# Layernorm's root and inverse as a power on GpSimd, and the recurrence's additions one pair later, in a two-layer transformer kernel

## The chip, the cores and the metric

The kernel runs on one core of a Trainium2 chip. The metric is the time of one execution on the device in microseconds (us), as the median of several runs. All arithmetic is in float32. Engines are called as in the profile: PE (TensorE), ACT (ScalarE), DVE (VectorE), POOL (GpSimd), SP (the engine that issues most DMAs).

## The reference, cut to what matters

```python
def _layernorm(x, axis=-1, eps=1e-05):
    m = jnp.mean(x, axis=axis, keepdims=True)
    v = jnp.var(x, axis=axis, keepdims=True)
    return (x - m) / jnp.sqrt(v + eps)

x = L0_attn_x                                       # (4, 2048, 256)
xn = _layernorm(x)
x = x + recurrence(xn) + attention_of_4_chosen_heads(xn)      # layer 0
xn = _layernorm(x)
x = x + causal_attention_16_heads(xn) + channel_mix(xn)       # layer 1
```

The recurrence is `y[t] = a[t] * y[t-1] + b[t]` over the 2048 tokens of a batch, with `a` and `b` from two matrix products, tanh, exp and a square root. The layer-0 attention takes the 4 best of 16 heads for each batch (64 columns each, 2048 by 2048 scores, softmax with the row's maximum subtracted). The layer-1 attention is causal, with 16 heads of 16 columns. The channel mix is `sigmoid(xr W_r) * (relu(xk W_k)^2 W_v)`, where `xr` and `xk` blend a token with the one before it.

## The kernel before, in words

**Order.** The whole program is traced under `in_order`, which ties each of PE, ACT, DVE and POOL to the order in which the Python code issues its instructions. So the order of the work on each engine is written out by hand: Python generators ("streams") are advanced by `steps(stream, count)`, each `yield` ending one step. DMAs on SP follow the order of issue too. The four batches run one after the other.

**Layer 0 attention, `attention0`.** A tile is 128 queries of one chosen head (`Tile0`), a pair is two tiles (`Pair0`). The loop runs over `n`, 0 to 33: pairs 0 to 31 (4 heads, 8 pairs each) and two more rounds that finish what is behind. In round `n` the pair `new` has tiles `a` and `c`; `before` is the pair of round `n-1`, `older` that of `n-2`. A round goes: transposes of the second tile of `before` (`late.turn`, L520, copied out of PSUM by `late.keep`, L526, two by DVE and two by ACT); reciprocals of its sums (L530, L531); output projection of `older` (`project`, L558) and its addition to `x` (`add`, L563); scores of `a` (L498) and their maxima on DVE (L502, combined by L506 into `nm`); exponentials of `a` on ACT (L512); scores of `c`; the product with the values of `before` (`weigh`, L545); exponentials of `c`; transposes of `a` and their copies. The start of a round can be seen in the trace as the `nm` (L506) of its tile `a`. Scores, transposes and projections take seven of the eight PSUM banks in turn, so each waits until the bank's previous user has been read.

Three streams are woven into these rounds. `background` is the recurrence of the same batch, of which 26 of 35 steps are done before round 0: the step for `y + added` of the second half (L330) and eight steps that transpose `y` (L337) and add it to `x` (L339) remain, at two steps a round. `rest_of_values` is the second half of the values' projection (`values0`, L446, copied by L448), four units in round 0. `norming` is `all_blocks`, from round 27 on, at four steps a round: the layernorm for layer 1, in four blocks of 512 tokens.

**Norm.** `stats` takes mean and variance of a tile of 128 tokens (L257, L258). `root` is a Sqrt on ACT with eps as bias (L261), `inverse` a reciprocal on DVE (L265), `rows` writes (x - mean) * inverse for each of four tiles (L272), and `turn` transposes 512 tokens by 128 columns (L278) and copies them (L279). In `all_blocks` a block takes eight steps, two rounds: root in the third, after the exponentials of `a`; inverse and rows in the fourth, after the copies of `a`; the two turns in the first two steps of the next round, one before `late.turn` and one after `late.keep`. Exp and Sqrt are in different tables of ACT, so a change of function is preceded by an ACT_TABLE_LOAD, which has the line of the instruction that it is for.

**Elsewhere.** Layer 0's norm is the same class: for batch 0 at the start of the program, for the others woven into the last head group of layer 1 of the batch before (`prepared`; two steps at a time), with one root and one inverse for all 16 tiles. In `opening1`, woven into the last rounds, `heads.open` fills tiles on POOL (L711, 128x2048) and `values1` fills others (L726); `heads.copy` then copies into them by DMAs from SP (L717). `Maxima` (L772, with L775 or L778) runs ahead for layer 1 in the same stage. In layer 1's late stage POOL also squares `ka` (L983) and adds `sg` (L1011).

Of the kernel before, what the change touches and what calls it, by code (L numbers as in the profile page):

```python
# [10 lines left out]
FP = mybir.dt.float32  # L11
BF = mybir.dt.bfloat16
U32 = mybir.dt.uint32
AF = mybir.ActivationFunctionType
ALU = mybir.AluOpType
# [3 lines left out]
P = 128  # L19
QB = 512  # L20
EPS = 1e-5
# [46 lines left out]
def steps(stream, count):  # L68

    for _ in range(count):  # L70
        if next(stream, StopIteration) is StopIteration:
            return False
    return True
# [3 lines left out]
def two_layers(ctx: ExitStack, tc: tile.TileContext, x, Wa, Wx, ba, bx, Lam,  # L77
# [4 lines left out]
    PE, ACT, DVE, POOL, SP = nc.tensor, nc.scalar, nc.vector, nc.gpsimd, nc.sync  # L82
# [3 lines left out]
    NT = T // P  # L86
    NQ = T // QB
# [7 lines left out]
    const = ctx.enter_context(tc.tile_pool(name="const", bufs=1))  # L95
# [37 lines left out]
    def rows_of(both, n, count):  # L133
# [13 lines left out]
    POOL.memset(cmask, 0.0)  # L147
    POOL.affine_select(out=cmask[:, QB - P:QB], in_=cmask[:, QB - P:QB], compare_op=ALU.is_ge, fill=MASKED,
                       base=0, pattern=[[-1, P]], channel_multiplier=1)
    eps_c = const.tile([P, 1], FP, tag="eps", name="eps_c")  # L150
    POOL.memset(eps_c, EPS)
    quarter_c = const.tile([P, 1], FP, tag="quarter", name="quarter_c")
    POOL.memset(quarter_c, 0.25)
    heads_row = const.tile([P, NH], FP, tag="heads_row", name="heads_row")
# [91 lines left out]
    class Norm:  # L246
# [10 lines left out]
            DVE.bn_stats(self.st[:, t, :], rows_of(self.xt, t, 1)[:, 0, :])  # L257
            DVE.bn_aggr(self.mv[:, t, :], self.st[:, t, :])  # L258

        def root(self, t, n):  # L260
            ACT.activation(self.rs[:, t:t + n], self.mv[:, t:t + n, 1:2].rearrange("p n o -> p (n o)"),  # L261
                           AF.Sqrt, bias=eps_c)

        def inverse(self, t, n):
            DVE.reciprocal(self.rs[:, t:t + n], self.rs[:, t:t + n])  # L265

        def rows(self, q, i0, i1):
            if i0 == 0:
# [182 lines left out]
    def queries0(b, k, xT, ch, bank):  # L451

        qs = [half_tile(f"q0_{b}_{k + i}") for i in range(2)]

        def stream():
            for q in range(NQ):
                blk = slice(q * QB, (q + 1) * QB)
                ps = bank()
                for c in range(2):
                    PE.matmul(ps, lhsT=ch.wq[k // 2][:, c, :], rhs=xT[c][:, blk], start=(c == 0), stop=(c == 1))  # L460
                ACT.activation(qs[0][:, blk], ps, AF.Identity, bias=ch.bias_q[:, k // 2:k // 2 + 1])
                for i in range(2):
                    SP.dma_start(qs[1][i * DH:(i + 1) * DH, blk], qs[0][(1 - i) * DH:(2 - i) * DH, blk])
                yield
        return qs, stream()

    def keys0(b, k, xT, ch, bank):

        kT = c4.tile([P, HT], FP, tag="k0", name=f"k0_{b}_{k}", bufs=2)

        def stream():
            for j in range(NJ):
                ps = bank()
                for c in range(2):
                    for i in range(2):
                        k0 = i * HT + j * QB
                        PE.matmul(ps[i * DH:(i + 1) * DH, :], lhsT=ch.wk[k][:, c, :], rhs=xT[c][:, k0:k0 + QB],  # L477
                                  start=(c == 0), stop=(c == 1))
                ACT.activation(kT[:, j * QB:(j + 1) * QB], ps, AF.Identity, bias=ch.bias[:, 1, k:k + 1])
                yield  # L480
        return kT, stream()
# [83 lines left out]
    def attention0(b, xT, xt, ch, recurring, first, v, rest_of_values, norm, opening, leading):  # L565


        NP = NT // 2
        qk, following = first, None
        background, projecting, norming = recurring, iter(()), iter(())  # L570
        older, before = None, None
        summing[0] = True

        def all_blocks():


            for q in range(NQ):
                yield
                yield
                norm.root(4 * q, 4)  # L580
                yield
                norm.inverse(4 * q, 4)
                norm.rows(q, 0, 2)
                norm.rows(q, 2, 4)
                yield
                for c in range(2):
                    norm.turn(q, c, ACT.copy)
                    yield
                yield
                yield  # L590

        for n in range(NA * NP + 2):
            k, i = divmod(n, NP)
            if i == 0 and 0 < k < NA:
                steps(projecting, 100)
                qk = following
            new = Pair0(b, k, i, *qk, v, xt) if k < NA else None
            a, c = new.tiles if new else (None, None)
            if i == NP - 3 and k + 1 < NA:
                if k % 2:  # L600
                    qs, querying = queries0(b, k + 1, xT, ch, bank)
                else:
                    qs, querying = qk[0], iter(())
                kT, keying = keys0(b, k + 1, xT, ch, bank)
                following = qs, kT
                projecting = concat(querying, keying)
            if n == (NA - 1) * NP + 3:
                norming = all_blocks()

            steps(background, 1)  # L610
            steps(projecting, 1)
            steps(norming, 1)

            if n in (NA * NP - 3, NA * NP - 1) or n >= NA * NP:
                steps(opening, 2)
            if n >= NA * NP:
                leading.lead()
            if before:
                late = before.tiles[1]
                late.turn(1)  # L620
                late.turn(0)
                late.keep(1, 0, DVE.tensor_copy)
                late.keep(0, 0, DVE.tensor_copy)
                late.keep(0, 1, ACT.copy)
                late.keep(1, 1, ACT.copy)
                for tile_ in before.tiles:
                    tile_.share()
            steps(background, 1)
            steps(projecting, 1)
            steps(norming, 1)  # L630
            if older:
                older.project()
                older.add()
                if n - 2 >= (NA - 1) * NP:
                    for t in range(2):
                        norm.stats(2 * (n - 2 - (NA - 1) * NP) + t)
            if before and new is None:
                leading.lead()
            if new:
                a.scores(0)  # L640
                a.scores(1)
                a.exponentials((0, 1))
                steps(rest_of_values, 4)
            steps(norming, 1)
            if new:
                c.scores(1)
            if n >= NA * NP:
                steps(opening, 1)
            if before:
                if new is None:  # L650
                    leading.lead()
                before.weigh(0)
            if new:
                c.scores(0)
                c.exponentials((1, 0))
            if before:
                if new is None:
                    leading.lead()
                before.weigh(1)
            if new:  # L660
                a.turn(1)
                a.turn(0)
                a.keep(1, 0, DVE.tensor_copy)
                a.keep(0, 0, DVE.tensor_copy)
                a.keep(1, 1, ACT.copy)
            if before:
                before.weighed()
            if new:
                a.keep(0, 1, ACT.copy)
            steps(norming, 1)  # L670
            older, before = before, new
        steps(background, 100)
        summing[0] = False
        for _ in range(8):
            steps(opening, 1)
            leading.lead()
            steps(norming, 1)
        steps(norming, 100)
# [336 lines left out]
    def prepared(b, ready):  # L1015

        xt = load_x(b)
        norm = Norm(xt, f"0_{b}", own_bank)
        ch = Chosen()
        ready.append((xt, norm.xT, ch))  # L1020

        def go():
            for t in range(0, NT, 2):
                norm.stats(t)
                norm.stats(t + 1)
                yield
            norm.root(0, NT)
            yield
            norm.inverse(0, NT)
            for q in range(NQ):  # L1030
                norm.rows(q, 0, 2)
                yield
                norm.rows(q, 2, 4)
                yield
                yield
                for c in range(2):
                    norm.turn(q, c, DVE.tensor_copy)
                    yield
        return go(), choose(b, norm.xT, ch)
# [3 lines left out]
    with in_order(tc):  # L1043
# [3 lines left out]
        for b in range(B):  # L1047
# [20 lines left out]
            x1, norm = xt, Norm(xt, f"1_{b}", bank)  # L1068
# [37 lines left out]
```

## Time and profile before

| | us |
|---|---|
| median of 3 runs | 4234.19 (4233.68 to 4235.58) |
| the profiled execution's own time | 4234.65 |
| its span, first to last instruction | 4232.9 |
| ACT table loads in it, 58 of 1.283 each | 74.4 |
| of these for the norms' Sqrt (L261), 20 | 25.7 |
| L506 to L506 of the same tile of the next round, rounds 6 to 10 | 11.82 |
| the same, rounds 27 and 29 | 15.78 |

The profile is of one execution. "Busy" is the time in which an engine ran instructions; the brackets at a row's end in a timeline are the idle time of the engine before it and what ended it. The stages of the four batches repeat almost to the hundredth of a microsecond, so one batch (the second, from about 1151 us) is read in detail, and times inside it are counted from the span's start.

### The profile page before, as it was taken

To read this page: it belongs to the slowest core of one execution; us is meant where nothing else is said; L and a number is where in the kernel's file an instruction comes from. 1 tells how busy PE (TensorE), PEld (TensorE's weight loads), DVE (VectorE), ACT (ScalarE), POOL (GpSimd) and SP (SyncE) were. 2 spreads that over 40 slices of the span, in tenths; PEclk is the share of its full clock that TensorE was granted. 3 is DMA by queue.
4 is the path that set the end of the run, shared out by engine and by line. 5 is a ranking of instruction groups with operands and counts; after the bars stand their busy time and mean duration, and the time that the engine had idled before them with its cause. 6 is when DMAs were issued, how large, how long until landed. Compare 5 with 4: busy or idle time off the path is not lost.

```text
span 4232.9 us, 86387 instructions
## 1 busy us (share of the span) xinstructions
PE 4129.7 (98%) x32994; PEld 2283.5 (54%) x32994; DVE 3107.5 (73%) x7292; ACT 2797.4 (66%) x6388; POOL 1044.9 (25%) x1322
## 2 busy tenths in 40 slices
PE   6999999999999999999999999999999999999998
PEld 3777643334477764333457776433446777643334
DVE  5777778887577777888657776888856767688882
ACT  3666648886566665888656665688865666568874
POOL 0000015544100002654410000265440000036544
PEclk9999999999999999999999999999999999999999
DMA  3000010100100001110010000011000000001000
GB/s 87 1 11 1 6 18 17 19 25 17 27 1 11 1 6 19 17 37 6 19 25 1 11 1 9 16 17 37 7 19 23 1 11 1 16 11 17 16 7 24
DMA packets 70819, 65.80 MB, mean 16 GB/s; under 512 B 37234, under 2 KB 58628, under 8 KB 68868
## 3 DMA queue, kind: packets, MB, share of 16 engines
q1 hardware_dynamic: 66624, 57.19, 6.2%
q8 instruction: 260, 4.26, 0.4%
q10 hardware_dynamic: 3780, 3.07, 0.3%
q14 instruction: 155, 1.27, 0.1%
HBM read 16.70 MB, written 8.39 MB: 6 GB/s over the span
## 4 chain that ended last, share of the span: by engine, by line
PE 90%; DVE 5%; ACT 2%; issue 1%; POOL 1%; DMA 1%; ACTq 0%; SPq 0%; POOLq 0%; DVEq 0%
PE bank L797 15%; PE bank L772 13%; PE bank L808 12%; PE bank L520 11%; PE bank L498 10%; PE bank L545 10%; PE bank L993 4%; PE bank L703 3%; PE bank L294 3%; PE bank L558 2%; DVE mx L778 1%; PE bank L477 1%; PE bank L460 1%; PE bank L981 1%; DVE mx L502 1%; ACT p L512 1%
## 5 line engine op out<-in xcount | busy, mean ns | idle before, releaser
L799 ACT ACTIVATE p<-bank 128x512 f32<-128x512 f32 (+3 forms) x2560 | 1175.4, 540 | 281.1 <-PE bank L797 146.5
L772 PE MATMUL bank<-k,q 32*128 32x512 f32 (+3 forms) x5120 | 1139.1, 564 | 3.2 <-DVE mx L778 1.3
L778 DVE TENSOR_REDUCE mx<-bank 128x1 f32<-128x512 f32 x1536 | 952.9, 682 | 239.0 <-PE bank L772 238.6
L797 PE MATMUL bank<-q,k 32*128 32x512 f32 (+3 forms) x5120 | 1089.6, 555 | 0.0
L512 ACT ACTIVATE p<-bank,nm 128x512 f32<-128x512 f32 x1024 | 689.5, 685 | 568.6 <-DVE nm L506 568.5
L815 POOL TENSOR_TENSOR o<-o,w 128x512 f32<-128x512 f32 (+3 forms) x576 | 627.6, 1090 | 757.5 <-ACT w L814 752.0
L502 DVE TENSOR_REDUCE mx<-bank 128x1 f32<-128x512 f32 x1024 | 645.3, 681 | 94.8 <-PE bank L498 94.2
L797 PEld LDWEIGHTS bank<-q,k 32*128 32x128 f32 x5120 | 418.4, 184 | 533.7 <-ACT p L799 445.5
L808 PE MATMUL bank<-p,v 128*17 128x512 f32 (+3 forms) x5120 | 602.9, 534 | 16.6 <-POOL p L802 11.7
L526 DVE COPY pT<-bank 128x512 f32<-128x512 f32 x512 | 352.6, 691 | 293.2 <-PE bank L520 277.6
L545 PEld LDWEIGHTS bank<-pT,v 128*64 128x64 f32 x8192 | 441.9, 137 | 189.8 <-issue 189.3
L498 PE MATMUL bank<-k,q 64*128 64x512 f32 x2048 | 542.5, 611 | 0.8
L775 DVE CUSTOM_DVE_ANT_0 bank<-bank,cmask 128x512 f32<-128x512 f32 (+3 forms) x1024 | 473.3, 521 | 75.0 <-PE bank L772 56.4
L520 PE MATMUL bank<-ident,p 128*128 128x128 f32 x4096 | 492.3, 275 | 19.9 <-ACT p L512 19.7
L545 PE MATMUL bank<-pT,v 128*64 128x128 f32 x8192 | 503.7, 276 | 0.0
L772 PEld LDWEIGHTS bank<-k,q 32*128 32x128 f32 x5120 | 426.7, 183 | 136.7 <-DVE mx L778 34.5
L520 PEld LDWEIGHTS bank<-ident,p 128*128 128x128 f32 x4096 | 445.3, 141 | 73.8 <-ACT p L512 29.8
L711 POOL MEMSET q<- 128x2048 f32 x16 | 28.9, 1804 | 1659.5 <-PE bank L545 1659.5
L814 ACT COPY w<-bank 128x512 f32<-128x512 f32 (+3 forms) x576 | 305.1, 530 | 101.9 <-PE bank L808 68.4
L526 ACT COPY pT<-bank 128x512 f32<-128x512 f32 x512 | 293.4, 600 | 63.5 <-PE bank L520 61.5
L808 PEld LDWEIGHTS bank<-p,v 128*17 128x17 f32 x5120 | 89.7, 95 | 431.1 <-ACT p L799 235.8
L498 PEld LDWEIGHTS bank<-k,q 64*128 64x128 f32 x2048 | 210.5, 188 | 170.7 <-issue 84.9
(164 smaller groups left out, 3354.8 us busy)
## 6 DMA issues: line engine op xcount, KB each, us to landing
x<-in_L_attn_x_dram SPq DMA_DIRECT2D x20, 512.0 KB
q<-q SPq DMA_DIRECT2D x64, 128.0 KB
vals<-o SPq DMA_DIRECT2D x256, 32.0 KB
out_dram<-x SPq DMA_DIRECT2D x32, 256.0 KB
q<-qp SPq DMA_DIRECT2D x48, 128.0 KB
k<-kp SPq DMA_DIRECT2D x48, 128.0 KB
q<-nmT SPq DMA_DIRECT2D x256, 2.0 KB
q<-qp SPq DMA_DIRECT2D x64, 32.0 KB
```

The costliest lines, as they stand in the source:

```text
L498: PE.matmul(self.s[j][i], lhsT=self.qT[i][half_, self.t * P:(self.t + 1) * P], rhs=self.kT[half_, j * QB:(j + 1) * QB], start=True, stop=True)
L502: DVE.tensor_reduce(self.mx[:, n:n + 1], self.s[j][i], AX.X, ALU.max)
L512: ACT.activation(self.p[j][:, i, :], self.s[j][i], AF.Exp, bias=nm, accum_out=self.sums[:, n:n + 1])
L520: PE.transpose(self.tr[j][i][:, n * P:(n + 1) * P], self.p[j][:, i, n * P:(n + 1) * P], ident)
L526: copy(self.pT[:, n0:n0 + 4, :], self.tr[j][i].rearrange("p (n q) -> p n q", q=P))
L545: PE.matmul(acc[i * DH:(i + 1) * DH, 0:P], lhsT=self.v[h][:, N * j + n, self.k * DH:(self.k + 1) * DH], rhs=tile_.pT[:, 8 * h + N * j + n, ...
L772: PE.matmul(s[:, 0:n], lhsT=self.qT[strip(h), self.qs], rhs=self.kT[strip(h), self.ks], start=True, stop=True)
L778: DVE.tensor_reduce(self.mx[:, h, :], s[:, 0:n], AX.X, ALU.max)
L797: PE.matmul(s[:, c0:QB], lhsT=self.kT[strip(h), self.ks], rhs=self.qT[strip(h), self.q0 + c0:self.q0 + QB], start=True, stop=True)
L799: ACT.activation(p[:, h % 2, c0:QB], s[:, c0:QB], AF.Exp, scale=SC1)
L808: PE.matmul(acc[32 * h:32 * h + DH1 + 1, c0:QB], lhsT=self.v[h], rhs=self.p[h // 2][:, h % 2, c0:QB], start=True, stop=True)
L815: POOL.tensor_tensor(self.o[:, c0:QB], self.o[:, c0:QB], w[:, c0:QB], ALU.add)
```

## The change

The norm's `root` method is gone. `inverse` now adds eps on DVE and raises the sum to the power -0.5 on POOL, in place. In `all_blocks` it stands where the root stood, in the third step, and `rows` stays in the fourth; for the first three blocks the two turns are put together behind `late.keep`, and the fourth keeps the old steps. In round 0 the recurrence's stream and half of the values' units are held back: the stream starts in round 1, and two of the four units come after the exponentials of `c`. 39 ACT_TABLE_LOADs fall out of the program with the 20 roots; one small tile of constants is set up in place of another.

```diff
-    eps_c = const.tile([P, 1], FP, tag="eps", name="eps_c")
-    POOL.memset(eps_c, EPS)
+    minus_half = const.tile([P, NT], FP, tag="minus_half", name="minus_half")
+    POOL.memset(minus_half, -0.5)
...
-        def root(self, t, n):
-            ACT.activation(self.rs[:, t:t + n], self.mv[:, t:t + n, 1:2].rearrange("p n o -> p (n o)"),
-                           AF.Sqrt, bias=eps_c)
-
         def inverse(self, t, n):
-            DVE.reciprocal(self.rs[:, t:t + n], self.rs[:, t:t + n])
+            rs = self.rs[:, t:t + n]
+            DVE.tensor_scalar(rs, self.mv[:, t:t + n, 1:2].rearrange("p n o -> p (n o)"), EPS, None, ALU.add)
+            POOL.tensor_tensor(rs, rs, minus_half[:, 0:n], ALU.pow)
...
             for q in range(NQ):
                 yield
                 yield
-                norm.root(4 * q, 4)
-                yield
                 norm.inverse(4 * q, 4)
+                yield
                 norm.rows(q, 0, 2)
                 norm.rows(q, 2, 4)
                 yield
+                if q < NQ - 1:
+                    yield
                 for c in range(2):
                     norm.turn(q, c, ACT.copy)
-                    yield
+                    if q == NQ - 1:
+                        yield
+                yield
                 yield
                 yield
...
-            steps(background, 1)
+            if n:
+                steps(background, 1)
...
-            steps(background, 1)
+            if n:
+                steps(background, 1)
...
-                steps(rest_of_values, 4)
+                steps(rest_of_values, 2)
...
                 before.weigh(1)
+            steps(rest_of_values, 2)
...
-            norm.root(0, NT)
+            norm.inverse(0, NT)
             yield
-            norm.inverse(0, NT)
             for q in range(NQ):
```

More of the change, by code (lines that the diff above doesn't have):

```diff
@@ L579, in all_blocks @@
                 yield
-                norm.root(4 * q, 4)
+                norm.inverse(4 * q, 4)
                 yield
-                norm.inverse(4 * q, 4)
                 norm.rows(q, 0, 2)
```

## The prediction

> **What bounds the kernel now.** First the page's engine shares:
>
> ```profile
> PE 4129.7 (98%) x32994; PEld 2283.5 (54%) x32994; DVE 3107.5 (73%) x7292; ACT 2797.4 (66%) x6388; POOL 1044.9 (25%) x1322
> ```
>
> PE's 98% is modelled and counts waits inside its pipeline, so I read the touched rounds instead. By windows (columns: length, then busy us of PE, weight loads, DVE, ACT, POOL, the granted clock, DMA), round 26 has no norm block and round 27 has one; otherwise they do the same:
>
> ```profile
> 1486.57:1499.44 12.87, 12.82 (x117) 8.95 (x117) 10.16 (x24) 7.78 (x21) 1.81 (x1) 1.00 0.01 2
> 1499.44:1515.22 15.78, 14.47 (x120) 10.02 (x122) 11.73 (x29) 11.61 (x26) 1.81 (x1) 1.00 0.00 1
> ```
>
> The block costs 15.78 - 12.87 = 2.91 us in this round. The timeline of ACT shows a hole of that size between the exponentials of tile a and those of tile c:
>
> ```profile
> 1502.26 0.21 ACT L512 ACTIVATION_READ_ACCUMULATOR p<-bank,nm 128x1 f32 x1
> 1502.49 1.28 ACT L261 ACT_TABLE_LOAD   x1
> 1503.79 0.30 ACT L261 ACTIVATE rs<-mv,eps_c 128x4 f32<-128x4 f32 x1
> 1504.10 1.28 ACT L512 ACT_TABLE_LOAD   x1
> 1505.40 0.69 ACT L512 ACTIVATE p<-bank,nm 128x512 f32<-128x512 f32 x1
> ```
>
> From 1502.49 to 1505.40 are 2.91 us: a round is a loop of latency, ACT's exponentials, PE's transposes, DVE's copies, additions and maxima, ACT again. DVE's timeline of the same round shows who waits:
>
> ```profile
> 1505.11 0.69 DVE L526 COPY pT<-bank 128x512 f32<-128x512 f32 x1 [0.18 <-PE bank L520]
> 1505.72 0.17 DVE L265 RECIPROCAL rs<-rs 128x4 f32<-128x4 f32 x1
> 1505.92 1.38 DVE L272 TENSOR_SCALAR xn<-x,mv,rs 128x256 f32<-128x256 f32 x4
> 1508.33 0.69 DVE L526 COPY pT<-bank 128x512 f32<-128x512 f32 x1 [1.03 <-PE bank L520]
> ```
>
> The rows lie inside the wait for ACT. Without the loads they are what is late next.
>
> **Rounds 27 and 29.** In round 26 the four copies start 4.80, 5.67, 6.54 and 7.42 us after its L506, each 0.18 behind PE. Without the loads, copies 1 and 2 stand at 4.80 and 5.67 again, the rows run from 6.30 to 7.68 (1.38), and copies 3 and 4, which PE has ready by then, follow back to back at 7.65 and 8.26, ending at 8.95 against 8.11. The round is 12.87 + 0.84 = 13.7, and 2.1 is gained. The turns (8 transposes, 1.0 us by L520's 3.71 for 32) now stand between late.turn and the projection: PE leaves late.turn at 7.74, the turns at 8.75, the projection (0.70) at 9.45, while DVE's additions are ready at 9.38: covered to within 0.1, and up to 0.5 dearer if their banks come late. Their two ACT copies (0.61 each) fall into ACT's 4 us wait for the next maxima.
>
> **Round 31.** There PE waited 1.23 for the exponentials of c behind the loads, then for rows, and L732 started 8.1 us after its L506. Without loads or an early turn, PE is through the transposes of a at 6.0: 2.1 gained. The later turns cost 0.5 beside DVE work that runs without a gap.
>
> So the three blocks give 2.1 + 2.1 + 2.1 = 6.3 a batch. The Exp load at L799 in the opening stage stands before an idle stretch of 3.15: nothing.
>
> **A rule on the loads.** The Trainium skill ("ScalarE: Activation LUTs", What ACT_TABLE_LOAD costs) puts a switch at 2.66 us with a drain of 1.38. The trace shows 1.283 and 0.02 between the last exponential and the load: no drain. By the page the hole would be 5.6 and the gain of a round 4.8; the round grew by only 2.91, so the row decides.
>
> **Round 0.** DVE's timeline of the second batch:
>
> ```profile
> 1143.49 2.47 DVE L330 TENSOR_SCALAR y<-y,added 128x2048 f32<-128x2048 f32 x2
> ...
> 1148.04 1.29 DVE L502 TENSOR_REDUCE mx<-bank 128x1 f32<-128x512 f32 x2 [1.31 <-PE bank L498]
> 1149.75 1.29 DVE L502 TENSOR_REDUCE mx<-bank 128x1 f32<-128x512 f32 x2 [0.42 <-PE bank L498]
> 1151.07 0.16 DVE L506 TENSOR_REDUCE nm<-mx 128x1 f32<-128x4 f32 x1
> ```
>
> PE sat idle for 4.73 before the y transposes at 1144.92, with the scores queued behind them, and then ran slowly (the last column but two is the clock):
>
> ```profile
> 1145.00:1150.00 5.00, 5.00 (x14) 2.12 (x15) 3.20 (x5) 0.00 (x0) 0.00 (x0) 0.54 0.01 3
> ```
>
> Now the scores follow the values at 1140.2 at full clock (1.99 instead of 3.78) and are ready early. DVE does one L330 (half of 2.47), to 1144.73, then four maxima (2.48): L506 at 1147.2, 3.9 earlier. Two values' units (1.8 each) then fill PE while ACT works; scores of c wait for the banks of a's exponentials until about 1150.2, the other two units end at 1153.8, the transposes of a at 1155.7. DVE copies (1.3), does the other L330 (1.24) to 1157.2, copies again (1.3), reciprocals (0.6), one L339 (0.7), and its maxima end at 1162.4. Before, round 1's L506 stood at 1169.03: 6.6 gained. What was moved is paid later: from L506 to L506 it is 12.78 into round 3 with two steps of the stream, 12.39 into round 4 with one, 11.82 into round 6 with none. Round 4 gets a second step (0.4), round 5 one beside the keys (0.6). Net 5.6 a batch. If PE still falls to the slow clock, the two units and c's scores cost up to 4 more: 1.6 to 5.6. SP's order is unchanged; no DMA moves.
>
> **The power.** The trace has none. POOL's two-input rows bound it:
>
> ```profile
> L815 POOL TENSOR_TENSOR o<-o,w 128x512 f32<-128x512 f32 x384 | 487.9, 1271 | 661.1 <-ACT w L814 659.5 <-ACT p L799 0.5
> ...
> L815 POOL TENSOR_TENSOR o<-o,w 128x128 f32<-128x128 f32 x64 | 29.1, 454 | 75.2 <-ACT w L814 75.2
> ```
>
> The line through them leaves 0.18 + 0.002 a column: 0.19 at the low end for 4 columns. A power as twenty such passes is 4, my high end. I take 0.4, near the 128x128 row. The addition on DVE is 0.16, in place of a 0.17 reciprocal. In rounds 27 to 31 the power starts 0.5 after L506 and is wanted at 6.30: 5.8 of cover. Were it later, L272 would hold DVE, and behind it copies 3 and 4, the reciprocals and the maxima that the next round starts from. The first fills of L711 (1490.80, 1503.65) now stand behind round 27's power; the second ends at 1505.46, 0.28 before the rows. For layer 0's 16 columns (three times), POOL is free at 1015.31 and DVE has 4.64 idle after the rows: cover to 5.3; PE is busy there without a gap, so the lost loads give nothing. At the start the rows come 0.3 earlier, since L219 holds DVE until 30.45 anyway.
>
> **Block four, and a rule against the change.** Here nothing lies between power and rows, and POOL's order puts two L711 fills behind the power. They ran early; now they are held until about 1598.5 and start as the rows become ready (timelines of POOL, DVE and PE):
>
> ```profile
> 1588.69 1.80 POOL L711 MEMSET q<- 128x2048 f32 x1 [20.50 <-PE bank L545]
> 1590.44 1.80 POOL L711 MEMSET k<- 128x2048 f32 x1
> ```
>
> ```profile
> 1598.42 1.38 DVE L272 TENSOR_SCALAR xn<-x,mv,rs 128x256 f32<-128x256 f32 x4
> ```
>
> ```profile
> 1598.89 1.30 PE L278 MATMUL bank<-ident,xn 128*128 128x128 f32 x4 [0.48 <-DVE xn L272]
> ```
>
> L272's own view (shortest, median, longest in ns) and a POOL timeline show what a POOL operation beside it does:
>
> ```profile
> L272 DVE TENSOR_SCALAR xn<-x,mv,rs x128: 400/407/1375, 30.9 to 3688.1; 128x256 f32<-128x256 f32 x128
> ```
>
> ```profile
> 1061.08 1.38 POOL L1011 TENSOR_TENSOR x<-x,sg 128x512 f32<-128x512 f32 x1 [1.75 <-DVE x L1010]
> ```
>
> A row takes 0.407, but up to 1.375, and the row begun at 1061.24, beside that L1011, ended just after it. No row lies beside a fill in the trace. By the rows seen beside POOL additions alone a writing fill could be free; the skill ("SBUF — State Buffer", Who interferes with whom) says that a tensor_scalar in a two-port mode and any POOL instruction shut each other out for the whole instruction. By the rule one row waits for each fill: 3.1 us more until the fourth row, PE waiting; without it, 0.2. I take 3.1, four times. The SP copies that need these tiles issue from about 1608; the fills end by 1602.3: covered by some 6.
>
> **Sum.** 4 x (6.3 + 5.6 - 3.1) + 0.3 = 35.5. Against the profiled execution (span 4232.9, own time 4234.65): span 4197.4, time 4199.1. The median of the runs is 0.46 lower: I say 4199.
>
> **Rivals.**
> 1. *The fills do not hold the rows* (10%). For: they only write. Against: the rule, and L272's 1375. Gain 35.5 + 4 x 2.9 = 47: 4187.
> 2. *Round 0 stays cold and the turns stand in PE's way* (20%). For: PE will still idle some 2 us behind a's exponentials, and the 0.1 of cover of the turns. Round 0 then gives 2.6 (three quarters of the way to the low end), the blocks 5.3 (0.5 twice): 4 x (2.6 + 5.3 - 3.1) = 19, so 4215.
> 3. *Another wait takes back what was won* (4%): 4226 to 4242. PE has no gap in the opening stage, but each round hands its start to the next, and no outside clock holds them, which speaks against it.
> 4. *Slower: the power is long* (6%). At a length d, block four pays d - 0.4 four times, rounds 27 and 29 d - 5.8 eight times, layer 0 d - 5.3 three times. 15d - 1.6 - 46.4 - 15.9 = 35.5 gives d = 6.6: from there on the kernel is slower; at 10 it is 4285. If 16 columns take four times as long, 4(d - 0.4) + 3(4d - 5.3) = 35.5 gives 3.3 for four columns. For: no row shows a power, and fixed cost need not be its main part. Against: twenty passes stay at 4.
> 5. *The change does not do what it says*: the Sqrt loads of the recurrence (L309) stay, but the 39 others have no cause left; under 1%, within case 3.
>
> The main case has 60%, by the sizes of 0.4 of power and of the fill 4192 to 4206. A long power short of case 4 (d = 3 costs 10) reaches 4210. The range takes in cases 1 and 2: 4184 to 4220. 0.2%, 8.5 us, is about what can be told from no change: faster 0.91, same 0.03, slower 0.06.
>
> **What would show it.** ACT_TABLE_LOADs at L261 gone and 19 left; L506 to L506 of 13.7 in rounds 27 and 29; L506 of rounds 0 and 1 15.2 apart instead of 17.96; two or more L272 in block four beside L711 at over 1.3 us; the power under 1 us on POOL. Wrong if rounds 27 and 29 keep 15, if PE's clock still falls to 0.54 in round 0, or if L272 of the early blocks waits for POOL.

## The result, and the profile after

The changed kernel takes 4215.39 us (median of 6 runs, 4215.05 to 4220.47) against 4234.47 (6 runs) for the kernel before: a ratio of 0.9959, 95% interval 0.9946 to 0.9971. It is 19 us faster. 4199.0 was predicted: the sign held, 4215 lies inside the range of 4184 to 4220, and the gain is little more than half of the 35.5 in the sum. The profiled execution has a span of 4213.5, 19.4 less than before. The kernel before took 4233.4 to 4234.5 beside every kernel of this document, so their times can be put side by side.

The page's engine shares moved little. ACT lost 52 us of busy time with 39 loads and 20 roots, and POOL gained 29 with the powers:

```profile
PE 4127.9 (98%) x32994; PEld 2290.6 (54%) x32994; DVE 3116.7 (74%) x7292; ACT 2745.6 (65%) x6329; POOL 1073.7 (25%) x1342
```

Rounds 26 and 27 of the second batch by windows (length, then busy us of PE, weight loads, DVE, ACT and POOL, the granted clock, DMA):

```profile
1475.17:1488.05 12.88, 12.82 (x117) 8.96 (x117) 10.16 (x24) 7.78 (x21) 0.00 (x0) 1.00 0.01 2
1488.05:1501.69 13.64, 13.59 (x124) 9.75 (x124) 11.36 (x30) 8.76 (x23) 4.60 (x3) 1.00 0.00 1
```

The round with the norm block now costs 0.76 more than the one without, where it cost 2.91. ACT's timeline has no hole between the exponentials of `a` and those of `c` any more, and on DVE the copies follow the rows back to back (in the changed kernel L510 are the exponentials, L524 the copies, L270 the rows):

```profile
1490.88 0.21 ACT L510 ACTIVATION_READ_ACCUMULATOR p<-bank,nm 128x1 f32 x1
1491.27 0.69 ACT L510 ACTIVATE p<-bank,nm 128x512 f32<-128x512 f32 x1 [0.18 <-DVE nm L504]
```

```profile
1493.72 0.69 DVE L524 COPY pT<-bank 128x512 f32<-128x512 f32 x1 [0.18 <-PE bank L518]
1494.33 1.37 DVE L270 TENSOR_SCALAR xn<-x,mv,rs 128x256 f32<-128x256 f32 x4
1495.62 1.28 DVE L524 COPY pT<-bank 128x512 f32<-128x512 f32 x2
```

The power, in the groups of POOL (busy us and mean ns after the bar):

```profile
L263 POOL TENSOR_TENSOR rs<-rs,minus_half 128x4 f32<-128x4 f32 x16 | 16.2, 1011 | 1895.7 <-DVE rs L262 1895.7
L263 POOL TENSOR_TENSOR rs<-rs,minus_half 128x16 f32<-128x16 f32 x4 | 11.7, 2930 | 24.0 <-DVE half_b L193 24.0
```

Four columns take 1.01 us and sixteen 2.93: by these two rows 0.37 plus 0.16 a column. 19 table loads are left, as predicted.

The stages, measured in both traces and put against the sum (us; a minus is a gain; the four values are batches 0 to 3):

| stage, for each batch | predicted | measured |
|---|---|---|
| start of the values to the first `nm` of round 0 | -3.9 | -3.9 in all four |
| round 0 (`nm` to `nm` of tile `a`; before 18.71, 17.96, 18.43, 18.62) | to 15.2 | 15.18, 18.03, 18.44, 18.20 |
| rounds 1 to 5 (before 65.66) | +1.0 | +1.1 |
| rounds 27 to 30 (before 64.18) | -4.2 | -4.3 |
| round 31 up to the block-four maxima | -2.1 | -2.4 |
| block four to the first exponential of layer 1 | +3.1 | +5.5, +6.1, +6.3, +6.1 |

Two rows fail. Round 0 came out as predicted in batch 0 alone, which leaves out about 3 us in each of three batches, 9 in all. Block four cost 2.4 to 3.2 more than its 3.1, nearly 12 in all. Together they are nearly 21, against a shortfall of 16 in the span. The difference came from elsewhere: round 31 gained 0.3 a batch more than said, round 0 of the kernel before was longer in the other three batches than in the second, which the prediction read (1.9 in all; that the four batches repeat to the hundredth does not hold for this round), and the rest of the program was shorter by about 1.5.

**Block four** in the second batch, on DVE, POOL and PE:

```profile
1579.81 0.17 DVE L262 TENSOR_SCALAR rs<-mv 128x4 f32<-128x4 f32 x1
1581.11 4.57 DVE L270 TENSOR_SCALAR xn<-x,mv,rs 128x256 f32<-128x256 f32 x4 [1.12 <-POOL rs L263]
```

```profile
1580.06 1.01 POOL L263 TENSOR_TENSOR rs<-rs,minus_half 128x4 f32<-128x4 f32 x1 [27.54 <-DVE rs L262]
1581.02 1.81 POOL L715 MEMSET q<- 128x2048 f32 x1
1582.76 1.81 POOL L715 MEMSET k<- 128x2048 f32 x1
```

```profile
1584.77 1.43 PE L276 MATMUL bank<-ident,xn 128*128 128x128 f32 x4 [4.43 <-DVE xn L270]
1585.99 3.62 PE L736 MATMUL bank<-wv,xT 128*128 128x256 f32 x8
```

The fills (now L715) stand just behind the power and run beside the rows, which take 4.57 for four instead of 1.38. PE waits 4.43 where it waited 0.48, and then its next eight matmuls take 3.62 instead of 1.89. The root and these eight matmuls in the kernel before:

```profile
1597.87 0.30 ACT L261 ACTIVATE rs<-mv,eps_c 128x4 f32<-128x4 f32 x1 [3.44 <-DVE mv L258]
```

```profile
1600.02 1.89 PE L732 MATMUL bank<-wv,xT 128*128 128x256 f32 x8
```

A window after the long wait of the changed kernel gives the clock, 0.50:

```profile
1585.00:1590.00 5.00, 5.00 (x16) 3.45 (x19) 2.22 (x11) 0.93 (x3) 0.00 (x0) 0.50 0.00 0
```

From the start of the stage's maxima to the end of these eight matmuls are 14.2 us against 8.4 before. The 5.8 more split into 3.2 for the fills (4.57 - 1.38), 0.75 for the way from variance to rows (1.30 from the addition's start, against 0.55 from the root's start before), and 1.8 for PE's slow stretch (4.84 from the first transpose to the end of the eight, against 3.02).

**Round 0** in the second batch, PE's timeline from just ahead of `nm` (1138.25), with the same wait of batch 0 ahead of it, and then a window of batch 0 and the same window of the second batch (batch 1):

```profile
102.26 2.46 PE L496 MATMUL bank<-k,q 64*128 64x512 f32 x6 [1.41 <-ACT p L510]
```

```profile
1136.74 1.12 PE L496 MATMUL bank<-k,q 64*128 64x512 f32 x2
1139.27 3.44 PE L496 MATMUL bank<-k,q 64*128 64x512 f32 x6 [1.41 <-ACT p L510]
1142.64 5.59 PE L444 MATMUL bank<-wv,xT 128*128 128x256 f32 x16
```

```profile
105.00:110.00 5.00, 5.00 (x33) 4.56 (x32) 2.11 (x5) 3.85 (x10) 0.00 (x0) 1.00 0.00 0
```

```profile
1142.00:1147.00 5.00, 5.00 (x14) 3.56 (x13) 1.54 (x3) 3.33 (x9) 0.00 (x0) 0.55 0.00 0
```

PE waits 1.41 us for the bank that `a`'s exponentials free, in both batches. After it, batch 0 goes on at clock 1.00 and batch 1 at 0.55, where the two units of the values take 5.59 instead of the 3.6 that the prediction had.

### The profile page after: what moved, and what is told of

Same layout as the page of the kernel before. It is cut to its first block, busy times and chain, and to the rows that moved or that the text cites. A ratio compares the mean times of both kernels' runs of the same rounds, so it can differ in the third digit from the quotient of the medians.

```text
span 4213.5 us, 86380 instructions
## 1 busy us (share of the span) xinstructions
PE 4127.9 (98%) x32994; PEld 2290.6 (54%) x32994; DVE 3116.7 (74%) x7292; ACT 2745.6 (65%) x6329; POOL 1073.7 (25%) x1342
## 4 chain that ended last, share of the span: by engine, by line
PE 89%; DVE 5%; issue 3%; POOL 1%; ACT 1%; DMA 1%; ACTq 0%; SPq 0%; POOLq 0%; DVEq 0%
PE bank L801 15%; PE bank L776 13%; PE bank L812 13%; PE bank L496 11%; PE bank L518 11%; PE bank L543 10%; PE bank L997 4%; PE bank L292 3%; PE bank L707 2%; PE bank L556 2%; PE bank L475 1%; PE bank L458 1%; PE bank L985 1%; DVE mx L500 1%; DVE mx L782 1%
## 5 line engine op out<-in xcount | busy, mean ns | idle before, releaser
L510 ACT ACTIVATE p<-bank,nm 128x512 f32<-128x512 f32 x1024 | 690.3, 686 | 545.4 <-DVE nm L504 494.2
L524 DVE COPY pT<-bank 128x512 f32<-128x512 f32 x512 | 351.4, 691 | 282.2 <-PE bank L518 263.8
L263 POOL TENSOR_TENSOR rs<-rs,minus_half 128x4 f32<-128x4 f32 (+1 forms) x20 | 27.9, 1395 | 1919.6 <-DVE rs L262 1895.7
L518 PE MATMUL bank<-ident,p 128*128 128x128 f32 x4096 | 483.7, 275 | 0.0
L524 ACT COPY pT<-bank 128x512 f32<-128x512 f32 x512 | 294.0, 600 | 80.2 <-PE bank L518 78.5
```

The lines of the kernel that those rows point to most:

```text
L510: ACT.activation(self.p[j][:, i, :], self.s[j][i], AF.Exp, bias=nm, accum_out=self.sums[:, n:n + 1])
L518: PE.transpose(self.tr[j][i][:, n * P:(n + 1) * P], self.p[j][:, i, n * P:(n + 1) * P], ident)
L524: copy(self.pT[:, n0:n0 + 4, :], self.tr[j][i].rearrange("p (n q) -> p n q", q=P))
```

## The experiments

Theory A: the gains of the norm blocks came as predicted and were given back in block four, where the power makes the fills meet the rows and leaves PE idle long enough to slow down; round 0 gives its full gain only where PE keeps its clock. Theory B: the blocks or the recurrence gained less than the sum says, or the later turns cost more. The first four kernels take the change apart; each is told against the change as made ("after") or the kernel before.

**The norm's part alone.** Round 0 as before, all the rest as after (the second guard, at the round's other call, is undone in the same way):

```diff
-            if n:
-                steps(background, 1)
+            steps(background, 1)
...
-                steps(rest_of_values, 2)
+                steps(rest_of_values, 4)
...
-            steps(rest_of_values, 2)
```

> The changed kernel with round 0 put back as it was before (recurrence's stream and all four units of the values at their old places), so the norm's part alone. My theory, from the stages of the two profiles: the stretch from the L506 of round 27 to that of round 31 keeps its gain (59.9 instead of 64.2 us in each batch), and the stretch from there to layer 1's first exponentials keeps its loss (about 81 instead of 77.5), because the two fills held behind the power stand beside the rows and PE then cools down. Left of the norm's part: 4 x (4.3 - 3.7), some 3 us with what else moves: about 4231. Rival, that the fills' loss came from round 0's shift of the whole batch: the loss in the opening stage goes away and the kernel takes about 4217.

Measured 4229.4 (13 runs, 4228.41 to 4231.81), ratio 0.999 (0.9982 to 0.9999, so only just clear of no change). The larger half of the change, 39 table loads of 1.283 us each, is worth 4 us: block four gives back almost all that rounds 27 to 31 win. From round 31 to the first exponential of layer 1 it takes 80.1 to 82.3 in place of 77.5, with round 0 as it was, so this loss is not a result of round 0's shift.

**The recurrence's part alone.** The kernel before, with only the guards `if n:` (there are two alike, one is shown) and the values' units two and two.

```diff
-            steps(background, 1)
+            if n:
+                steps(background, 1)
...
-                steps(rest_of_values, 4)
+                steps(rest_of_values, 2)
...
+            steps(rest_of_values, 2)
```

> The kernel before with round 0's part alone (stream one round later, two of the four units of the values after the exponentials of c). My theory: the first L506 of every batch 3.9 us earlier, L506 of rounds 0 to 1 at 15.2 in a batch where PE's clock holds and about 18 where it falls to 0.55, rounds 1 to 6 dearer by 1.1; with one batch of four warm: 4 x (3.9 - 1.1) + 3 = 14, about 4220. Rival, that round 0's gain needs the norm's part (fewer table loads on ACT before it): no gain over 5 us, 4229 or more.

Measured 4219.55 (6 runs, 4217.99 to 4221.03), ratio 0.9966 (0.9954 to 0.9978). So most of the 19 us is this part's: 14 alone, with round 0 at 15.18, 18.22, 18.10 and 18.01, short in one batch of four again. From round 31 to the first exponential of layer 1 it takes 77.46 in all four batches, as before. The losses there belong to the norm's part.

**The fills ahead of the power.** In the opening stage the two fills of the second head group (`heads.open(1, ...)`) are issued at `q == 2`, well before POOL gets block four's power:

```diff
         for q, count in enumerate((0, 3, 3, 2)):
+            if q == 2:
+                for i in range(2):
+                    heads.open(1, i)
...
-        for i in range(2):
-            heads.open(1, i)
         heads.copy(1, slice(0, T))
```

> The changed kernel, with the two POOL fills of the second head group (heads.open(1, ...)) asked for one step group earlier in the opening stream, so that they stand ahead of the fourth block's power in POOL's order and not behind it. My theory (the fills shut the rows out, and PE cools down in the wait): the four rows of the fourth block back from 4.57 to about 1.4 us, PE's wait before L276 from 4.43 to under 1.5, L736 behind it back from 3.6 to 1.9; 4 x 5.1 = 20 us faster than the changed kernel, about 4195. Rival, that the power itself (1.01 us and its two hand-overs) is what PE waits for: the rows shorten but PE's wait stays over 3, under 5 us in all, 4210 or more.

Measured 4193.98 (4 runs, 4192.01 to 4197.82), ratio 0.991 (0.9894 to 0.9925): 21 us faster than after. From round 31 to layer 1 it takes 75.8 to 76.5 in place of 80.6 to 81.3. PE's timeline of block four in the second batch has a wait of 1.23 ahead of the first transposes, and the eight matmuls behind them are back at full speed:

```profile
1576.71 1.30 PE L276 MATMUL bank<-ident,xn 128*128 128x128 f32 x4 [1.23 <-DVE xn L270]
1577.84 1.89 PE L736 MATMUL bank<-wv,xT 128*128 128x256 f32 x8
```

The fills beside the rows are the cause of block four's loss, and of the slow clock behind the long wait. That the rows wait was predicted; the clock's part was not. 0.75 of the loss stays: 1.23 of waiting against 0.48 before. Between the two profiled executions are 23.2 us; 20.3 of them lie in this stage and the other 3 in round 0, where two batches kept their clock instead of one.

**The values' units at their old place.** After, with all four units ahead of `a`'s exponentials again, the recurrence still a round later:

```diff
-                steps(rest_of_values, 2)
+                steps(rest_of_values, 4)
...
-            steps(rest_of_values, 2)
```

> The changed kernel with all four units of the values after the exponentials of tile a in round 0, as before; the recurrence's stream still starts in round 1. My theory (PE idles 1.4 us behind two units and a half-done pair of scores, and its clock falls in three batches of four): PE has no gap between scores and values, the clock stays at 1.00 in all batches, L506 of rounds 0 to 1 is 14.1 to 15.2 in all four instead of 15.2, 18.0, 18.4, 18.2; 9 to 14 us faster than the changed kernel, about 4204. Rival, that the 18 us come from waits for banks and not from the clock: the later scores of c make round 0 longer by up to 3 us in the batches, 4215 to 4225.

Measured 4206.04 (5 runs, 4205.22 to 4206.8), ratio 0.9935 (0.9921 to 0.9948): 9 us faster than after. Round 0 takes 14.80 in all four batches. The units fill the wait, what is left of it is 0.74, and a window of the second batch, at the same point of the round, shows the full clock:

```profile
1133.95 5.45 PE L444 MATMUL bank<-wv,xT 128*128 128x256 f32 x24
1140.14 1.99 PE L444 MATMUL bank<-wv,xT 128*128 128x256 f32 x8 [0.74 <-ACT p L510]
```

```profile
1140.00:1145.00 5.00, 4.86 (x25) 3.16 (x26) 2.48 (x5) 3.05 (x9) 0.00 (x0) 1.00 0.00 2
```

Holding the values back was itself the mistake: it left the hole of 1.41 behind which the clock fell.

**One fill ahead, one in place.** This asks how the rows and the fills share their time: a fill for each row, or the first row behind all of them.

```diff
+            if q == 2:
+                heads.open(1, 0)
...
-        for i in range(2):
-            heads.open(1, i)
+        heads.open(1, 1)
```

> The changed kernel with only one of the two fills of the second head group (the q tile) moved ahead of the fourth block's power; the k tile's fill stays behind it. My theory (a row that starts beside a fill is shut out until the fill ends; in the changed kernel the first row took 3.61 us, the length of both fills): the first row 1.8 us, the four rows about 2.8 instead of 4.57, PE's wait before L276 about 2.6, short enough for part of the batches to keep the clock; 2 to 4 us a batch faster than the changed kernel, 4199 to 4208. Rival (one row is held per fill, whichever comes first, or the wait is the power's): rows at 3.0 or more or unchanged at 4.5, 4210 or more.

Measured 4205.04 (5 runs, 4200.9 to 4206.37), ratio 0.9929 (0.9916 to 0.9943), between after and the kernel with both fills ahead. The view of the rows' line (shortest, median, longest in ns), of after and of this kernel:

```profile
L270 DVE TENSOR_SCALAR xn<-x,mv,rs x128: 394/406/3607, 30.1 to 3667.3; 128x256 f32<-128x256 f32 x128
```

```profile
L270 DVE TENSOR_SCALAR xn<-x,mv,rs x128: 394/406/1866, 29.9 to 3658.3; 128x256 f32<-128x256 f32 x128
```

With two fills one row lasts 3.607 (about two fills of 1.8), with one 1.866. The first row stands behind both fills that follow each other on POOL, and not, as the prediction had it, one row behind each. The sum comes out the same. PE's wait ahead of L276 is 2.7 in each batch; in three the clock fell and the time from round 31 to layer 1 is 78.5 to 78.6, in the fourth it held and the time is 77.3. So here the slow clock alone costs 1.2 to 1.4.

**The turns at their old places.** After, with the turns of the first three blocks one ahead of `late.turn` and one behind `late.keep`, as before:

```diff
                 yield
-                if q < NQ - 1:
-                    yield
                 for c in range(2):
                     norm.turn(q, c, ACT.copy)
-                    if q == NQ - 1:
-                        yield
-                yield
+                    yield
                 yield
                 yield
```

> The changed kernel with the two turns of blocks one to three at their old places, one ahead of late.turn and one behind late.keep. My theory (the rows end 7.7 us after L506, and a turn ahead of late.turn holds PE and the copies 3 and 4 until then): rounds 27 and 29 about 1 us longer than 13.64, block three as before; 4 x 2 to 4 x 3, so 4223 to 4227. Rival (PE has the turn's time to spare, the grouping of the turns is worth nothing): rounds 27 and 29 within 0.2 of 13.64, 4215.

Measured 4233.15 (13 runs, 4232.1 to 4235.21), ratio 0.9999 (0.999 to 1.0007). All of the gain is gone, 6 us beyond the edge of what was expected. Rounds 27 and 29 take 15.24 instead of 13.64, since PE now waits for the rows ahead of `late.turn`, which the whole round follows:

```profile
1502.63 1.21 PE L276 MATMUL bank<-ident,xn 128*128 128x128 f32 x4 [0.83 <-DVE xn L270]
```

A wait for the rows was expected, but at about 1 us a round; it is 1.6, so 13 us in all instead of 8. The other part of the miss is block three, which was expected as in the changed kernel: its first turn now stands behind the transposes of round 31, with the same wait of 0.83, and from round 31 to layer 1 the time is 82.2 to 83.4, on average 1.5 a batch more. So the power by itself gains little in rounds 27 and 29 (15.24 against 15.78). With the turns where they were the wait only passes from ACT's load to PE, and the later turns are what lets the round shorten.

**Both repairs, and the same kernel again.** The edits of the third and the fourth kernel together; the second measurement, on another chip, asks whether PE's clock falls in the same batches again.

> Fills ahead of the power and all four units of the values at their old place together. My theory (two independent losses): rows of block four at 1.4, L506 of rounds 0 to 1 at 14.8 in all four batches, so the 75.8 us from round 31 to layer 1 and the 14.8 add up: about 4186. Rival (both cures are one, since a colder clock in one place sets the state of the other): no better than the better of the two, 4192 or more.

> The same kernel as e7, once more beside e8. If PE's clock after the short wait of the fourth block is a matter of chance from batch to batch, the batches that fall (77.5 instead of 75.8 from round 31 to layer 1) need not be those of e7, and the times spread over some 5 us, 4182 to 4189; if the order of the work sets it, the same three batches fall and the spread stays under 2 us around 4188.

Measured 4188.29 (4 runs, 4184.84 to 4188.94), ratio 0.9889 (0.9874 to 0.9904), and 4186.26 (4 runs, 4185.87 to 4186.57), ratio 0.9888 (0.9871 to 0.9904). From round 31 to layer 1 the first has 77.45, 75.82, 77.45 and 77.46 in its four batches, the second 75.80, 77.43, 75.81 and 76.25: the same code, and other batches at the slower value. Batch 0 of the first has the wait that the third kernel had too:

```profile
541.47 1.29 PE L276 MATMUL bank<-ident,xn 128*128 128x128 f32 x4 [1.23 <-DVE xn L270]
542.60 3.19 PE L735 MATMUL bank<-wv,xT 128*128 128x256 f32 x8
```

Its clock behind the wait (0.57), and then that of the third kernel at the same place of the same batch (1.00):

```profile
543.00:547.00 4.00, 4.00 (x15) 2.18 (x14) 0.92 (x6) 1.03 (x3) 0.00 (x0) 0.57 0.00 0
```

```profile
546.00:550.00 4.00, 4.00 (x22) 2.16 (x21) 2.34 (x9) 1.57 (x4) 0.00 (x0) 1.00 0.00 0
```

A wait of 1.23 is thus enough for the clock to fall, but not in each batch. Which batch it is has to do with the moment at which the wait comes (the last section).

**Root and inverse of block four on ACT and DVE.** If the remaining wait of 1.23 is the power's, it goes when block four alone keeps the Sqrt and the reciprocal. POOL then has no power there, so the fills stay at their place; the values' units are at their old place. The constant `eps_c` comes back too and is left out here.

```diff
+        def root(self, t, n):
+            ACT.activation(self.rs[:, t:t + n], self.mv[:, t:t + n, 1:2].rearrange("p n o -> p (n o)"),
+                           AF.Sqrt, bias=eps_c)
+
+        def invert_root(self, t, n):
+            DVE.reciprocal(self.rs[:, t:t + n], self.rs[:, t:t + n])
...
-                norm.inverse(4 * q, 4)
+                if q < NQ - 1:
+                    norm.inverse(4 * q, 4)
+                else:
+                    norm.root(4 * q, 4)
                 yield
+                if q == NQ - 1:
+                    norm.invert_root(4 * q, 4)
...
-                steps(rest_of_values, 2)
+                steps(rest_of_values, 4)
...
-            steps(rest_of_values, 2)
```

> The changed kernel with all four units of the values at their old place in round 0 (as in e4), and with the fourth block's root and inverse on ACT and DVE as before the change (eight table loads come back, where ACT is idle); the fills stay at their place and have no power ahead of them. My theory (in the fourth block only the path from the statistics to the rows counts: 0.6 us by ACT against 1.3 by POOL, and PE's wait of 1.2 before L276 still lets the clock fall in three batches of four of e7): PE's wait back to 0.5, L736 at 1.9 in every batch, round 31 to layer 1 at 75.2 in all four against 77.5, 75.8, 77.5, 77.5 in e7; 4180. Rival (the loads cost what they did in the earlier blocks, 2.9 us, because ACT's copies of the values stand behind them): no better than e7, 4187 or more.

Measured 4179.97 (4 runs, 4179.57 to 4180.9), ratio 0.9873 (0.9857 to 0.989): 53 us faster than the kernel before, 35 faster than after, and 6 faster than the kernel with both repairs, measured on the same chip. Round 31 to layer 1 takes 75.06 in all four batches. On ACT the load for the root falls into a stretch in which ACT waits for the variances anyway; on PE the wait is the 0.48 of before and the clock holds:

```profile
1565.53 1.28 ACT L263 ACT_TABLE_LOAD   x1
1570.25 0.30 ACT L263 ACTIVATE rs<-mv,eps_c 128x4 f32<-128x4 f32 x1 [3.44 <-DVE mv L260]
```

```profile
1571.26 1.30 PE L285 MATMUL bank<-ident,xn 128*128 128x128 f32 x4 [0.48 <-DVE xn L279]
```

A load that nobody waits for is cheaper than the power that took its place: here 3.44 us of idle time are left on ACT after it.

## Why the prediction was right in part and wrong in size

Two terms of the sum were too favourable: round 0 was put at 5.6 a batch and gave 2.7 to 3.2 in three batches of four, and block four was put at a loss of 3.1 and lost 5.5 to 6.3. The other terms held to about 0.3 a batch.

- **Rounds 27 and 29: right.** 13.7 said, 13.64 measured, by the mechanism given: no hole on ACT, the rows next in line, the copies behind them. The turns ahead of the projection were covered, as said; the sixth experiment shows that 1.6 of the 2.1 gained hang on them.
- **Round 31: right.** 2.1 said, 2.4 measured, and by the mechanism given: PE's wait of 1.23 for the exponentials is gone, and the transposes of `a` end 6.0 after the `nm`, as said.
- **Start of round 0: right.** The first `nm` comes 3.9 earlier in every batch, and rounds 1 to 5 pay 1.1 for the moved steps (1.0 said).
- **Round 0 itself: the step that failed is "scores of c wait for the banks of a's exponentials ... the other two units end at 1153.8".** The wait was named, and the work behind it was costed at full clock. That held in one batch of four. In the others PE ran on at about 0.55 and the round kept its 18 us; the prediction had named this as a sign of being wrong ("if PE's clock still falls to 0.54 in round 0"). The wait of 1.41 is the same in all four; that batch 0 came out as said was luck, since the moment of the wait decided it (the last section). The prediction gave the low end of this term ("up to 4 more: 1.6 to 5.6") and took the high one. Measured: 6.3 in batch 0 and 2.7 to 3.2 in the other three, counted as the prediction did (start, round 0, moved steps).
- **Block four: right mechanism, wrong size.** 3.1 a batch said, 5.8 measured in the stage itself. The rule of the Trainium skill ("SBUF — State Buffer", Who interferes with whom), that a DVE tensor_scalar in a two-port mode and a POOL instruction shut each other out, held for the rows and the fills: 3.2 measured. Mis-sized or missing were the power's own way, 0.75 of which 0.2 was counted (its 1.01 was taken for 0.4), and the slow matmuls after PE's wait, 1.8. The prediction said "PE waiting" and then costed only the wait.
- **The power elsewhere: covered, as said.** 1.01 and 2.93 us stay under the covers of 5.8 and 5.3, though four columns take more than twice the 0.4 that was assumed and just miss the sign "under 1 us". Rival 4 needed 3.3 us or more for four columns.
- **Rival 2** comes to the measured time, 4215. Of its two halves, round 0 staying cold is what the trace shows, in three batches of four; turns in PE's way is not, since the rounds are at 13.64. Its number is right because it left block four at 3.1 and lowered the blocks by 1.0 instead. That agreement is partly chance.
- **Not what took the gain:** layer 0's lost loads give nothing, as said, and no new wait of size arose in rounds 1 to 30 (rounds 6 to 26 are 0.1 to 0.2 longer in all).

In both failed terms the larger missing piece is the same: a wait of PE can cost more than its own length, since the work behind it may run at a lower clock.

## What to carry to other kernels

When an operation is moved to another engine, read that engine's queue behind it: the power was short and hidden, but it held two fills back until they met the rows. Before moving work off a path, look at each place where it runs: in rounds 27 to 31 the loads stood in the loop, in block four they stood in idle time, and replacing them there lost what the others won. And cost a wait on PE together with the matmuls after it, at full and at half clock, even where the wait is only a little over one microsecond.

## What the runs showed of the hardware that was not expected

- **PE's clock after short waits.** Behind waits of 1.41 us (round 0) and 1.23 us (block four) the granted clock was 0.55 to 0.57 in some batches and 1.00 in others, with the same instructions and the same wait. Behind waits of 0.48 and 0.74 it stayed at 1.00 in the windows looked at.

The clock's record in the traces shows what differs. Within one execution all falls begin a whole number of steps of 3.4133 us apart (those of the changed kernel at 1139.65 and 2180.71 lie 305 steps apart). Here are the steps around the wait of 1.41, of batch 0 and then of batch 1:

```profile
98.59:102.00 3.41, 2.26 (x8) 1.02 (x6) 3.38 (x8) 0.57 (x1) 0.00 (x0) 1.00 0.00 0
102.00:105.41 3.41, 3.15 (x10) 1.57 (x11) 2.60 (x5) 2.69 (x9) 0.00 (x0) 1.00 0.00 0
```

```profile
1136.24:1139.65 3.41, 2.00 (x6) 0.76 (x5) 3.33 (x7) 1.21 (x3) 0.00 (x0) 1.00 0.00 0
1139.65:1146.48 6.83, 6.83 (x15) 4.15 (x14) 2.32 (x5) 4.86 (x16) 0.00 (x0) 0.50 0.00 1
1146.48:1149.89 3.41, 3.41 (x25) 3.15 (x25) 1.52 (x3) 1.15 (x2) 0.00 (x0) 1.00 0.00 0
```

In batch 0 the edge of a step divides the wait into 1.15 and 0.26, and the clock holds. In batch 1 the whole wait lies in one step, and the clock is at half for the next two. The five traces with this wait (the changed kernel and the second, third, fifth and sixth experiments) have it in 20 batches. In 14 it lies in one step (once but for 0.02 us), the clock falls at the end of that step and the round takes over 18 us; in the other six an edge divides it, the clock holds and the round takes 15.18.

For the wait of 1.23 in block four this is not enough: in the three traces that have it the clock fell in four batches of twelve, all with a wait that begins 0.62 to 0.95 us into a step, and held in five others whose wait also lies wholly in one step but begins elsewhere. The kernel before waits 1.23 in rounds 27, 29 and 31, and its clock never fell there. What else counts within a step stays open, and no experiment moved the steps on purpose.

The Trainium skill ("TensorE: Matmul & The Clock Gate", Part 1: The HAM clock gate) has the clock fall after at least one idle window of about 3.4 us. It also says that the window runs freely, so that the same kernel can differ from run to run. The steps fit the window, and the batches that change between the two measurements of one kernel fit a window that runs freely. A whole idle window was not needed here: 1.41 us in one step were enough, and in block four of the changed kernel's batch 0 the clock fell 1.80 us into the wait of 4.43.

- **Fills in a row.** The DVE row that meets two fills standing behind each other on POOL waits for both: 3.607 us, against 1.866 with one. That need not hold for every POOL instruction: in the kernel before, two rows beside two L983 of 1.04 each, one behind the other, took 0.587 and 1.126, so one waited for each.
- **A power on POOL** costs 1.01 us for 128x4 and 2.93 for 128x16. It grows by 0.16 a column, which the additions read for the prediction (0.002 a column) did not suggest.
